# Products with w2 of 17 expert groups by one level of Strassen's algorithm

## The chip, the cores and the metric

The kernel runs on one core of a Trainium2 chip, in fp32 throughout. The metric is the device time of one execution in microseconds (us). The time before is the median of three executions. The profile is one execution, taken by the hardware profiler.

## The reference

One layer: a graph step with a dense 4096 x 4096 adjacency matrix, then a transformer block with a mixture of experts. The change concerns only the last loop.

```python
# x: 4096 x 256, adj: 4096 x 4096
x = x + gnn(layernorm(x), adj, neigh_W, lin_W)
x = x + ffn(layernorm(x), ...)          # the block below

# ffn: causal attention of 4 heads, then
flat = rmsnorm(x, ln2_w)                 # 4096 x 256
probs = softmax(flat @ router_w.T)       # 8 experts
tp, ti = top_k(probs, 2)                 # each token has two experts
for e in range(8):                       # hidden width 682
    hh = silu(flat @ w1[e].T) * (flat @ w3[e].T)
    out = out + weights[:, e:e+1] * (hh @ w2[e].T)
return x + out
```

## The kernel before

The kernel runs in three stages. First it multiplies the adjacency matrix with the features; there it already uses one level of Strassen's algorithm in Winograd's form, with the sums on VectorE (lines 374 to 377 and 444 to 450). Then it does attention with routing: each token's row is scattered into the list of each of its two experts. The third stage, from about 1109 us, does the experts, and the change is here.

Experts are worked off in groups of rows of one expert's list. There are 25 whole groups of 256 rows (numbers below `NW`) and 17 small ones of 128 rows that are done in the usual run. `TURNS` sets the order: nine whole groups first, then whole and small ones mixed so that each kind is spread evenly, then three whole ones. Written out, W for whole and s for small, from k = 0 to k = 41:

```
WWWWWWWWW sWsWsWssWsWsWsWssWsWsWssWsWsWs WWW
```

The program fixes the order on each engine by the order in which the code emits its instructions. For each k the main loop emits `hidden(k)`, then `combine(k - 1)`, with the loads of later groups between them.

`hidden(k)` makes 11 blocks of 128 hidden channels (5 of w1, 5 of w3, and one that holds both tails of 42 channels) from xT, the transposed rows, in three steps q = 0, 2, 4 with 8, 8 and 6 products (line 1105). Each step has its own PSUM pool of the three in `p_sc`. ScalarE takes silu (line 1111), VectorE multiplies (line 1112) into hT; the tail is multiplied last (line 1122). After the step q = 0 it calls `prepare(k + 1)`, which transposes the next group's rows (line 1083) into a tile tx of the pool `p_y` and copies it from there to xT on ScalarE (line 1088).

`combine(k)` multiplies hT and tail with w2 (line 1150): for each half of 128 rows six products, each with 128 channels of hT as stationary operand and 128 x 256 of w2 moving. Their sums lie in a tile ye of the pool `p_y`, which has a single buffer of one bank: tx and ye take turns in it. VectorE works out the gate (pick and gt, lines 1134 and 1138) and scales the sums to y (line 1161); GpSimd adds y to the rows in DRAM with an indirect DMA (line 1166). The last two groups use a bank of `p_ms` as well, one for each half.

One fp32 product shows as two matmul records in the profile.

Loads go through the queue of SyncE in the order of the code: for each k the weights w1 and w3 of k + 3 (`load13`, line 1053), the rows of k + 4 (`load_rows`, line 1069) and w2 of k + 2 (`load2`, line 1059). w13 and w2 have three places each; the rows have five buffers, of which one comes free when the scatter of its group has landed. `rest` holds what is left of routing and is worked off by `step()` in the first iterations.

Of the kernel before, what the change touches and what calls it, by code (L numbers as in the profile page):

```python
# [9 lines left out]
F32 = mybir.dt.float32  # L10
I32 = mybir.dt.int32
SP = mybir.EngineType.SP
AF = mybir.ActivationFunctionType
ALU = mybir.AluOpType
# [3 lines left out]
P = 128  # L18
N = 4096
C = 256  # L20
# [6 lines left out]
NF = 5  # L27
TAIL = HID - NF * P
T0 = 64
# [12 lines left out]
GR = 256  # L42
SM = 128
NA = -((NE * (GR - 1) - 2 * (N - 512)) // GR)
NW = -((NE * (GR - 1) - 2 * N) // GR)
# [8 lines left out]
NM = NG - RARE  # L54
# [12 lines left out]
def fast_kernel(  # L67
# [24 lines left out]
    nc = tc.nc  # L92
# [85 lines left out]
    kT = [kvp.tile([P, 512], F32, name=f"kT{b}") for b in range(NB)]  # L178
# [38 lines left out]
    with (  # L217
# [81 lines left out]
        T3 = G12  # L299
        HC = C // 2  # L300
# [230 lines left out]
    with (  # L531
# [259 lines left out]
                join(put, "late writes")  # L791


        def after(b):

            return [
                [None, lambda: inputs(b)],
                [None],
                [lambda: project(b, 0)],
                [lambda: project(b, 1)],  # L800
                [lambda: turn(b, 0)],
                [lambda: turn(b, 1), lambda: residual(b)],
                [lambda: logits(b)],
                [lambda: weigh(b)],
                [None, lambda: choose(b)],
                [None, lambda: scaled(b, 0)],
                [None, lambda: scaled(b, 1)],
                [lambda: place(b), lambda: scaled(b, 2)],
                [None, lambda: scaled(b, 3), lambda: scatter(b, 0, 0)],
                [None, lambda: scatter(b, 0, 1), lambda: scatter(b, 1, 0)],  # L810
                [None, lambda: scatter(b, 1, 1), lambda: scatter(b, 2, 0)],
                [None, lambda: scatter(b, 2, 1), lambda: scatter(b, 3, 0)],
                [None, lambda: scatter(b, 3, 1)],
            ]


        def last_qkv():
            b, made = NB - 1, {}

            def scales():  # L820
                stats(ax, b)
                var = mv[b][:, :, 1:2]
                power(rstd[b], var, 1.0, EPS_LN)
                power(both[b], var, *BOTH)

            def norm():
                made["h0"] = ax.tile([P, TB, ROW], F32, tag="row", name="h0_l")
                for t in range(TB):
                    normed(made["h0"][:, t, 0:C], b, t, both[b][:, t])

                made["hT"] = qT[b]

            def turned(h):
                tr = p_ms.tile([P, 2, 2, P], F32, tag="ms", name=f"tr_l{h}")
                for t in range(2):
                    for c in range(2):
                        nc.tensor.transpose(
                            tr[:, c, t, :], made["h0"][:, 2 * h + t, c * P : (c + 1) * P], ident
                        )
                for c in range(2):  # L840
                    nc.scalar.activation(
                        made["hT"][:, c, h * 2 * P : (h + 1) * 2 * P],
                        tr[:, c].rearrange("p t i -> p (t i)"),
                        AF.Copy, scale=ln1_sb[:, c : c + 1],
                    )

            def rotate(t):
                pj = p_ms.tile([P, 512], F32, tag="ms", name=f"pq_l{t}")
                room = ex.tile([P, NF, GR], F32, tag="hT", name=f"ro_l{t}")
                ro, r2 = (  # L850
                    room.rearrange("p k i -> p (k i)")[:, k : k + 384].rearrange(
                        "p (h s d) -> p h s d", s=2, d=HD // 2
                    )
                    for k in (0, 384)
                )
                rotated(ax, b, t, made["hT"], pj, ro, r2, cos_l[:, t, None, :], sin_l[:, t, None, :])
                made[t] = ro

            def turn_heads(t):
                tr = p_ms.tile([P, 2, 2, P], F32, tag="ms", name=f"trq_l{t}")  # L860
                heads(b, t, made.pop(t), tr)

            return [
                [None, scales], [None, norm], [lambda: turned(0)], [lambda: turned(1)],
                [lambda: rotate(0)], [lambda: rotate(1)],
                [lambda: turn_heads(0)], [lambda: rotate(2)],
                [lambda: turn_heads(1)], [lambda: rotate(3)],
                [lambda: turn_heads(2)], [lambda: turn_heads(3)],
                *guard(),
            ]  # L870
# [157 lines left out]
                join(put, "pads")  # L1028


        tails = [eg.tile([P, GR], F32, name=f"tail{n}") for n in range(2)]
        for t in tails:
            nc.gpsimd.memset(t, 0.0)

        at13 = (qT_all[:, 0 : 2 * W13], qT_all[:, 2 * W13 : 4 * W13], res_all[:, 0 : 2 * W13])
        W2 = (NF + 1) * C
        at2 = (
# [39 lines left out]
        def prepare(k, pool=p_y, tag="y"):  # L1077
# [13 lines left out]
                )  # L1091
            inputs_of[i] = xT

        def hidden(k, step=None, behind=None):
            i = TURNS[k]
            n = halves(i) * P
            w13_sb, xT = w13s[k % 3], inputs_of.pop(i)
            hT = ex.tile([P, NF, n], F32, tag="hT", name=f"hT_{i}")

            for q in range(0, NF + 1, 2):  # L1100
                ps = next(p_sc).tile([P, 2, 2, GR], F32, tag="sc", name=f"h_{i}_{q}")
                ps = ps[:, :, :, 0:n]
                for m in range(2 * q, min(2 * q + 4, 2 * NF + 1)):
                    for c in range(2):
                        nc.tensor.matmul(  # L1105
                            ps[:, m % 2, m // 2 - q, :], w13_sb[:, c, m * P : (m + 1) * P],
                            xT[:, c, :], start=(c == 0), stop=(c == 1),
                        )
                both = 2 if q + 1 < NF else 1
                si = ax.tile([P, 2, n], F32, tag="rden", name=f"si_{i}_{q}")  # L1110
                nc.scalar.activation(si[:, 0:both, :], ps[:, 0, 0:both, :], AF.Silu)  # L1111
                nc.vector.tensor_mul(  # L1112
                    hT[:, q : q + both, :], si[:, 0:both, :], ps[:, 1, 0:both, :]
                )
                if q == 0 and behind is not None:
                    prepare(behind)
                if step and q < NF - 1:
                    step()

            nc.scalar.activation(si[T0 : T0 + TAIL, 1, :], ps[0:TAIL, 0, 1, :], AF.Silu)  # L1120
            tail = tails[k % 2][:, 0:n]
            nc.vector.tensor_mul(
                tail[T0 : T0 + TAIL, :], si[T0 : T0 + TAIL, 1, :], ps[T0 : T0 + TAIL, 0, 1, :]
            )
            hidden_of[i] = (hT, tail)

        def combine(k):
            i = TURNS[k]
            n = halves(i)
            w2_sb = w2s[k % 3]  # L1130
            hT, tail = hidden_of.pop(i)
            r = rows.pop(i)
            pick = ex.tile([P, n, NE], F32, tag="pick", name=f"pick_{i}")
            nc.vector.tensor_mul(
# [4 lines left out]
            y = ax.tile([P, HALF, C], F32, tag="yT1", name=f"y_{i}")  # L1139

            last = k >= NM - 2
            ps = [
                pool.tile([P, HALF, C], F32, tag=tag, name=f"ye_{i}_{tag}")
                for pool, tag in ((p_ms, "ms"), (p_y, "y"))[0 if last else 1 :]
            ]

            def products(h):
                cols = slice(h * P, (h + 1) * P)
                for q in range(NF + 1):
                    nc.tensor.matmul(  # L1150
                        ps[h if last else 0][:, h, :],
                        hT[:, q, cols] if q < NF else tail[:, cols],
                        w2_sb[:, q, :], start=(q == 0), stop=(q == NF),
                    )

            for h in range(0 if last else n):
                products(h)
            for h in range(n):
                if last:
                    products(h)  # L1160
                nc.vector.tensor_scalar(  # L1161
                    y[:, h, :], ps[h if last else 0][:, h, :], gt[:, h], None, op0=ALU.mult
                )
                at = bass.IndirectOffsetOnAxis(ap=r[:, h, C : C + 1].bitcast(I32), axis=0)
                nc.gpsimd.memset(gap, 0.0)
                put = nc.gpsimd.indirect_dma_start(  # L1166
                    out=(acc_dram if k < NM - LAST else out)[:, :],
                    out_offset=at,
                    in_=y[:, h, :], in_offset=None, compute_op=ALU.add,
                )  # L1170
                if h:
                    free(put, f"half {i}", "an expert has a token once")
                else:
                    join(put, f"half {i}")
                if i < NA:
                    free(put, "last x", "the tokens of the first groups are others")
                    join(put, "first sums")
# [816 lines left out]
```

## Time and profile before

| | |
|---|---|
| time, median of three | 1638.8 us (1638.38 to 1639.15) |
| span of the profiled execution | 1636.5 us |
| TensorE busy | 1603.5 us |
| VectorE busy | 928.8 us |
| ScalarE busy | 457.9 us |
| line 1105, products of hidden(), wide groups' xT in qT_all | 220.5 us |
| line 1150, products with w2, largest row | 99.8 us |
| mean DMA rate | 128 GB/s |

How to read it: the engine rows are the union of the times in which at least one instruction of the engine ran; rows of a line likewise. TensorE is the engine with nearly no idle time. The chain of waits, followed back from the end, lies on PE for 88% of the span and on VectorE for 6%. Of the span, 10% are in this chain on line 1150. In the list of waits a line reads "engine, line, what it waited for: us in total, times, longest".

### The profile page before, as it was taken

What the parts mean: (1) busy time and instruction counts of PE and PEld (TensorE: products, weight loads), DVE (VectorE), ACT (ScalarE), POOL (GpSimd) and SP (SyncE); (2) the same over time, 40 slices, a digit from 0 to 9 for tenths busy, and PEclk for the clock granted to TensorE, in tenths of its full rate; (3) what the DMA queues carried; (4) which work ended last, traced back from release to release, by engine and by line L of the source; (5) the groups of instructions that cost most, each with busy time, mean ns of one, the idle gap of its engine ahead of it and who ended that gap; (6) DMA issues with size and microseconds to landing.
All of it is one profiled execution on the core that took longest, in us unless ns stands there. A gap on an engine that the chain in (4) does not pass through costs nothing.

```text
span 1636.5 us, 24754 instructions
## 1 busy us (share of the span) xinstructions
PE 1603.5 (98%) x9588; PEld 1157.6 (71%) x9588; DVE 928.8 (57%) x1914; ACT 457.9 (28%) x866; POOL 405.0 (25%) x604
## 2 busy tenths in 40 slices
PE   7999999999999999999999999999999999999997
PEld 5669999999999534344343434338888998999986
DVE  5647756756666578779778888793432222222221
ACT  2110000100000445555555455553211121221120
POOL 1001211111112221352434323412422222222122
PEclk9999999999999999999999999999999999999999
DMA  6224434434433000010001000066756777777765
GB/s 225 73 76 158 141 144 141 152 131 157 158 133 133 4 1 1 17 37 27 30 25 40 28 13 28 20 204 212 239 164 207 233 248 233 226 254 225 234 213 144
DMA packets 67711, 209.73 MB, mean 128 GB/s; under 512 B 14656, under 2 KB 46272, under 8 KB 53952
## 3 DMA queue, kind: packets, MB, share of 16 engines
q1 hardware_dynamic: 54320, 190.05, 33.4%
q0 software_dynamic: 12720, 17.47, 5.6%
q8 instruction: 78, 1.28, 0.3%
q10 hardware_dynamic: 544, 0.52, 0.1%
q14 instruction: 49, 0.40, 0.1%
HBM read 180.81 MB, written 31.42 MB: 130 GB/s over the span
## 4 chain that ended last, share of the span: by engine, by line
PE 88%; DVE 6%; issue 2%; ACT 2%; POOL 1%; DMA 1%; DVEq 0%; SPq 0%; ACTq 0%; POOLq 0%
PE acc L423 24%; PE h L1105 20%; PE ya L590 11%; PE sc L555 11%; PE ye_y L1150 10%; PE pf L385 3%; PE pq L184 3%; DVE sum L578 3%; PE po L624 2%; ACT pt L560 1%; PE tx L1083 1%; PE dn L603 1%; PE tr L318 1%; PE trq L212 1%; PE pq_l L184 0%
## 5 line engine op out<-in xcount | busy, mean ns | idle before, releaser
L560 ACT ACTIVATE pt<-sc 128x1024 f32<-128x1024 f32 (+3 forms) x288 | 251.8, 957 | 201.1 <-PE sc L555 162.5
L578 DVE TENSOR_TENSOR sum<-sum,pt 128x1024 f32<-128x1024 f32 (+3 forms) x258 | 294.3, 1141 | 20.4 <-POOL pt L562 0.5
L555 PE MATMUL sc<-qT_all,kT 64*128 64x512 f32 (+3 forms) x1152 | 253.3, 573 | 6.1 <-ACT pt L560 5.3
L423 PE MATMUL acc<-g,a 128*128 128x128 f32 x2048 | 255.7, 275 | 0.0
L590 PE MATMUL ya<-pt,vv 128*64 128x512 f32 (+3 forms) x1152 | 242.6, 563 | 0.0
L423 PEld LDWEIGHTS acc<-g,a 128*128 128x128 f32 x2048 | 241.8, 192 | 0.0
L1105 PE MATMUL h<-xT,qT_all 128*128 128x256 f32 (+1 forms) x1232 | 220.5, 335 | 0.0
L1112 DVE TENSOR_TENSOR hT<-si,h 128x256 f32<-128x256 f32 (+2 forms) x126 | 64.0, 508 | 261.1 <-ACT si L1111 261.1
L1105 PEld LDWEIGHTS h<-xT,qT_all 128*128 128x128 f32 x1232 | 194.2, 191 | 18.9 <-issue 1.0
L555 PEld LDWEIGHTS sc<-qT_all,kT 64*128 64x128 f32 x1152 | 104.2, 187 | 143.0 <-issue 105.1
L590 PEld LDWEIGHTS ya<-pt,vv 128*64 128x64 f32 x1152 | 76.3, 136 | 144.6 <-issue 138.7
L1166 POOL DMA_INDIRECT acc_dram<-y,rows x61 | 96.1, 1575 | 332.4 <-DVE y L1161 328.1
L1111 ACT ACTIVATE si<-h 128x256 f32<-128x256 f32 (+2 forms) x126 | 57.2, 454 | 376.3 <-PE h L1105 376.2
L1105 PE MATMUL h<-xT,res_all 128*128 128x256 f32 (+1 forms) x616 | 114.6, 342 | 0.0
L1105 PEld LDWEIGHTS h<-xT,res_all 128*128 128x128 f32 x616 | 100.3, 191 | 10.2 <-issue 0.2
L423 PE MATMUL acc<-g,more_sums 128*128 128x129 f32 (+1 forms) x768 | 101.7, 275 | 0.6 <-DVE more_sums L376 0.6
L423 PEld LDWEIGHTS acc<-g,more_sums 128*128 128x128 f32 x768 | 94.6, 192 | 7.5 <-issue 7.5
L1150 PE MATMUL ye_y<-res_all,hT 128*128 128x256 f32 x430 | 99.8, 379 | 0.0
L782 POOL DMA_INDIRECT lists<-row,slots x64 | 69.1, 1080 | 109.1 <-issue 106.5
L1150 PEld LDWEIGHTS ye_y<-res_all,hT 128*128 128x128 f32 x430 | 80.9, 190 | 10.5
L1161 DVE TENSOR_SCALAR y<-ye_y,gt 128x256 f32<-128x256 f32 x65 | 29.3, 481 | 86.1 <-PE ye_y L1150 86.0
L423 PE MATMUL acc<-g,qT_all 128*128 128x128 f32 (+1 forms) x512 | 74.0, 274 | 0.0
(231 smaller groups left out, 1716.5 us busy)
## 6 DMA issues: line engine op xcount, KB each, us to landing
a<-in_adj_dram SPq DMA_DIRECT2D x64, 1024.0 KB, 4.9
qT_all<-in_w_dram SPq DMA_DIRECT2D x28, 1408.0 KB, 8.2
res_all<-in_w_dram SPq DMA_DIRECT2D x28, 768.0 KB, 5.1
res_all<-in_w_dram SPq DMA_DIRECT2D x14, 1408.0 KB, 7.5
qT_all<-in_w_dram SPq DMA_DIRECT2D x14, 768.0 KB, 4.9
rows<-lists SPq DMA_DIRECT2D x25, 265.0 KB, 2.8
lists<-pad SPq DMA_DIRECT2D x8, 662.5 KB, 14.1
res_all<-in_x_dram SPq DMA_DIRECT2D x8, 512.0 KB, 9.4
```

The lines of the kernel that those rows point to most:

```text
L184: nc.tensor.matmul(pj, hT[:, c, t * P : (t + 1) * P], wqkv_sb[:, c, :], start=(c == 0), stop=(c == 1),)
L423: nc.tensor.matmul(acc[t][bank][:, at : at + w], m[left][:, k, t * P : (t + 1) * P], g[jb][:, right, k, 0:w], start=(jb == 0 and k == 0 an ...
L555: nc.tensor.matmul(ps[:, j, :w], kT[sb][hd, i * P : (i + 1) * P], qT[b][hd, p, off:], start=True, stop=True,)
L560: nc.scalar.activation(pt[:, :, :w], ps[:, :, :w], AF.Exp, scale=HD ** -0.5)
L578: nc.vector.tensor_add(sums[b, p][:, :, off:], before[:, :, off:], pt[:, :, : 512 - off])
L590: nc.tensor.matmul(accs[b, p][hd, off:], vv[sb][:, i, hd], pt[:, j, : 512 - off], start=(s == 0), stop=(s == TB * b + TB - 1),)
L782: put = nc.gpsimd.indirect_dma_start(out=lists[:, :], out_offset=bass.IndirectOffsetOnAxis(ap=chosen[b][:, k, t, :], axis=0), in_=flats[b] ...
L1105: nc.tensor.matmul(ps[:, m % 2, m // 2 - q, :], w13_sb[:, c, m * P : (m + 1) * P], xT[:, c, :], start=(c == 0), stop=(c == 1),)
L1111: nc.scalar.activation(si[:, 0:both, :], ps[:, 0, 0:both, :], AF.Silu)
L1112: nc.vector.tensor_mul(hT[:, q : q + both, :], si[:, 0:both, :], ps[:, 1, 0:both, :])
L1150: nc.tensor.matmul(ps[h if last else 0][:, h, :], hT[:, q, cols] if q < NF else tail[:, cols], w2_sb[:, q, :], start=(q == 0), stop=(q == NF),
L1166: put = nc.gpsimd.indirect_dma_start(out=(acc_dram if k < NM - LAST else out)[:, :], out_offset=at, in_=y[:, h, :], in_offset=None, comput ...
```

## The change

For 17 of the 25 whole groups (k = 6 to 39, where `TURNS[k] < NW`) the products with w2 are done by one level of Strassen's algorithm in Winograd's form. The matrix of 256 rows by 768 channels (six chunks of 128, the last one padded with zeros) is cut into four parts: by halves of rows and by even and odd chunks. w2 is cut by even and odd chunks and by halves of output channels. Seven products of three chunks each, 128 columns wide, take the place of eight; 15 sums on VectorE and one copy on ScalarE make this good.

- The tile hT gets a sixth chunk for the tail, and two fixed tiles hTs take the place of the rotating hT and of the tails. The rotation of the last block's heads borrows the same tiles.
- `split(k)`, at the end of `hidden(k)`, makes four sums of hT and four of w2, each 128 x (3 x 128), on VectorE. They lie in tiles of the attention stage that are no longer needed (kT and vv); two are written in place, over parts of hT and w2.
- `seven_products(k)`, in `combine(k)`, makes the products: four into a bank of `p_ms`, three into the one of `p_y`, and adds them up.
- The scaling of y with the gate goes to ScalarE for these groups.
- `prepare` of the next group moves from after q = 0 to after q = 2, in every group.

```diff
+        hTs = [eg.tile([P, NF + 1, GR], F32, name=f"hT{n}") for n in range(2)]
+        for t in hTs:
+            nc.gpsimd.memset(t[:, NF, :], 0.0)
...
-                room = ex.tile([P, NF, GR], F32, tag="hT", name=f"ro_l{t}")
+                room = hTs[t % 2]
...
-        tails = [eg.tile([P, GR], F32, name=f"tail{n}") for n in range(2)]
-        for t in tails:
-            nc.gpsimd.memset(t, 0.0)
...
+        SEVEN = [k for k in range(6, NM - 2) if TURNS[k] < NW]
+        def split(k, hT):
...
+                chunks = hT.rearrange("p (j c) i -> p c j i", c=2)[:, c]
+                weights = w2_sb.rearrange("p (j c) o -> p c j o", c=2)[:, c]
+                for h in range(2):
+                    m[f"A{h + 1}{c + 1}"] = chunks[:, :, h * P : (h + 1) * P]
+                    m[f"G{c + 1}{h + 1}"] = weights[:, :, h * P : (h + 1) * P]
+            first = k % 2 * 3
+            for n, s in enumerate(("S1", "S2", "S4")):
+                m[s] = kT[first + n][:, 0 : 3 * P].rearrange("p (j i) -> p j i", j=3)
+            for n, s in enumerate(("T1", "T2", "T4")):
+                m[s] = vv[first + n][:, 0:3, :]
+            m["S3"], m["T3"] = m["A21"], m["G12"]
+            nc.vector.tensor_add(m["S1"], m["A21"], m["A22"])
+            nc.vector.tensor_sub(m["S2"], m["S1"], m["A11"])
+            nc.vector.tensor_sub(m["S4"], m["A12"], m["S2"])
+            nc.vector.tensor_sub(m["S3"], m["A11"], m["A21"])
+            nc.vector.tensor_sub(m["T1"], m["G12"], m["G11"])
+            nc.vector.tensor_sub(m["T3"], m["G22"], m["G12"])
+            nc.vector.tensor_sub(m["T2"], m["G22"], m["T1"])
+            nc.vector.tensor_sub(m["T4"], m["T2"], m["G21"])
...
+        def seven_products(k):
...
+            banks = [
+                pool.tile([P, 4, HC], F32, tag=tag, name=f"ye_{i}_{tag}")
+                for pool, tag in ((p_ms, "ms"), (p_y, "y"))
+            ]
+            for number, left, right in (
+                (1, "A11", "G11"), (2, "A12", "G21"), (6, "S2", "T2"), (7, "S3", "T3"),
+                (5, "S1", "T1"), (3, "S4", "G22"), (4, "A22", "T4"),
+            ):
+                n = len(p)
+                p[number] = banks[n // 4][:, n % 4, :]
+                for j in range(3):
+                    nc.tensor.matmul(
+                        p[number], m[left][:, j, :], m[right][:, j, :],
+                        start=(n % 4 == 0 and j == 0), stop=(j == 2), skip_group_check=True,
+                    )
...
+            nc.scalar.copy(u2, p[1])
+            nc.vector.tensor_add(c[0][:, 0], u2, p[2])
+            nc.vector.tensor_add(u2, u2, p[6])
+            nc.vector.tensor_add(u3, u2, p[7])
+            nc.vector.tensor_add(u4, u2, p[5])
+            nc.vector.tensor_add(c[0][:, 1], u4, p[3])
+            nc.vector.tensor_sub(c[1][:, 0], u3, p[4])
+            nc.vector.tensor_add(c[1][:, 1], u3, p[5])
...
         def hidden(k, step=None, behind=None):
...
-                if q == 0 and behind is not None:
+                if q == 2 and behind is not None:
                     prepare(behind)
...
-            hidden_of[i] = (hT, tail)
+            hidden_of[i] = hT
+            if k in SEVEN:
+                split(k, hT)
...
         def combine(k):
...
+            if seven:
+                done = seven_products(k)
...
+                if seven:
+                    nc.scalar.activation(
+                        y[:, h, :], done[h].rearrange("p h o -> p (h o)"), AF.Copy, scale=gt[:, h]
+                    )
+                else:
+                    nc.vector.tensor_scalar(
+                        y[:, h, :], ps[h if last else 0][:, h, :], gt[:, h], None, op0=ALU.mult
+                    )
```

More of the change, by code (lines that the diff above doesn't have):

```diff
@@ L1092, in prepare @@
             inputs_of[i] = xT
+        SEVEN = [k for k in range(6, NM - 2) if TURNS[k] < NW]
+        parts_of = {}
+        def split(k, hT):
+            w2_sb = w2s[k % 3]
+            m = {}
+            for c in range(2):
+                chunks = hT.rearrange("p (j c) i -> p c j i", c=2)[:, c]
[17 more added lines that the diff above has]
+            nc.vector.tensor_sub(m["T4"], m["T2"], m["G21"])
+            parts_of[k] = m
@@ new lines, in seven_products @@
+        def seven_products(k):
+            i = TURNS[k]
+            m = parts_of.pop(k)
+            HC = C // 2
+            banks = [
+                pool.tile([P, 4, HC], F32, tag=tag, name=f"ye_{i}_{tag}")
+                for pool, tag in ((p_ms, "ms"), (p_y, "y"))
+            ]
+            p = {}
+            for number, left, right in (
[9 more added lines that the diff above has]
+                    )
+            c = [vv[6 + k % 2].rearrange("p (r h) o -> p r h o", r=2)[:, r] for r in range(2)]
+            u2 = u4 = c[0][:, 1]
+            u3 = c[1][:, 1]
+            nc.scalar.copy(u2, p[1])
[6 more added lines that the diff above has]
+            nc.vector.tensor_add(c[1][:, 1], u3, p[5])
+            return c
@@ L1097, in hidden @@
             w13_sb, xT = w13s[k % 3], inputs_of.pop(i)
-            hT = ex.tile([P, NF, n], F32, tag="hT", name=f"hT_{i}")
+            hT = hTs[k % 2][:, :, 0:n]
             for q in range(0, NF + 1, 2):
@@ L1120, in hidden @@
             nc.scalar.activation(si[T0 : T0 + TAIL, 1, :], ps[0:TAIL, 0, 1, :], AF.Silu)
-            tail = tails[k % 2][:, 0:n]
             nc.vector.tensor_mul(
-                tail[T0 : T0 + TAIL, :], si[T0 : T0 + TAIL, 1, :], ps[T0 : T0 + TAIL, 0, 1, :]
+                hT[T0 : T0 + TAIL, NF, :], si[T0 : T0 + TAIL, 1, :], ps[T0 : T0 + TAIL, 0, 1, :]
             )
-            hidden_of[i] = (hT, tail)
+            hidden_of[i] = hT
+            if k in SEVEN:
+                split(k, hT)
         def combine(k):
@@ L1130, in combine @@
             w2_sb = w2s[k % 3]
-            hT, tail = hidden_of.pop(i)
+            hT = hidden_of.pop(i)
             r = rows.pop(i)
@@ L1141, in combine @@
             last = k >= NM - 2
[L1142 to L1145, printed above, removed]
+            seven = k in SEVEN
+            if seven:
+                done = seven_products(k)
+            else:
+                ps = [
+                    pool.tile([P, HALF, C], F32, tag=tag, name=f"ye_{i}_{tag}")
+                    for pool, tag in ((p_ms, "ms"), (p_y, "y"))[0 if last else 1 :]
+                ]
             def products(h):
@@ L1151, in products @@
                         ps[h if last else 0][:, h, :],
-                        hT[:, q, cols] if q < NF else tail[:, cols],
-                        w2_sb[:, q, :], start=(q == 0), stop=(q == NF),
+                        hT[:, q, cols], w2_sb[:, q, :], start=(q == 0), stop=(q == NF),
                     )
-            for h in range(0 if last else n):
+            for h in range(0 if last or seven else n):
                 products(h)
@@ L1160, in combine @@
                     products(h)
-                nc.vector.tensor_scalar(
-                    y[:, h, :], ps[h if last else 0][:, h, :], gt[:, h], None, op0=ALU.mult
-                )
+                if seven:
+                    nc.scalar.activation(
+                        y[:, h, :], done[h].rearrange("p h o -> p (h o)"), AF.Copy, scale=gt[:, h]
+                    )
+                else:
+                    nc.vector.tensor_scalar(
+                        y[:, h, :], ps[h if last else 0][:, h, :], gt[:, h], None, op0=ALU.mult
+                    )
                 at = bass.IndirectOffsetOnAxis(ap=r[:, h, C : C + 1].bitcast(I32), axis=0)
```

## The prediction

> **What bounds the kernel now.** I read the engine table of the page first, then its clock row, then the list of who waited for whom, then the timeline of the stretch that the change touches.
>
> ```profile
> PE 1603.5 (98%) x9588; PEld 1157.6 (71%) x9588; DVE 928.8 (57%) x1914; ACT 457.9 (28%) x866; POOL 405.0 (25%) x604
> PEclk9999999999999999999999999999999999999999
> ```
>
> TensorE is busy 98% of the span at full clock. In the expert stage (from about 1180 us) the list of waits has no entry of PE or PEld at all. So here each us that TensorE is spared comes off the time, and each us that it is made to wait goes on it. What matters is not the share of VectorE (a quarter in this stage: 86.5 of the 343.1 us from 1246.4 to 1589.5) but where its work stands in its order. One pair of a small and a whole group, timeline of before (start, length, engine, line, operation; a count of weight loads on PEld):
>
> ```profile
> 1350.91 2.03 PEld L1150 LDWEIGHTS ye_y<-res_all,hT 128*128 128x128 f32 x10
> ...
> 1355.98 3.43 PEld L1105 LDWEIGHTS h<-xT,qT_all 128*128 128x128 f32 x16
> ...
> 1356.40 0.88 DVE L1161 TENSOR_SCALAR y<-ye_y,gt 128x256 f32<-128x256 f32 x2 [3.55 <-PE ye_y L1150]
> ...
> 1365.70 2.13 PEld L1150 LDWEIGHTS ye_y<-qT_all,hT 128*128 128x128 f32 x10
> ...
> 1367.39 0.42 DVE L1122 TENSOR_TENSOR tail<-si,h 42x256 f32<-42x256 f32 x1 [0.44 <-ACT si L1120]
> 1367.85 0.17 DVE L1134 TENSOR_TENSOR pick<-rows,mine 128x8 f32<-128x8 f32 x1
> ...
> 1368.05 0.16 DVE L1138 TENSOR_REDUCE gt<-pick 128x1 f32<-128x8 f32 x1
> ...
> 1368.29 1.97 PEld L1105 LDWEIGHTS h<-xT,res_all 128*128 128x128 f32 x16
> ...
> 1368.71 0.48 DVE L1161 TENSOR_SCALAR y<-ye_y,gt 128x256 f32<-128x256 f32 x1 [0.49 <-PE ye_y L1150]
> ...
> 1370.18 0.47 PEld L1083 LDWEIGHTS tx<-ident,rows 128*128 128x128 f32 x4
> ...
> 1374.42 0.38 SPq L1069 DMA_DIRECT2D rows<-lists  x1
> ...
> 1375.04 0.33 SPq L1059 DMA_DIRECT2D qT_all<-in_w_dram  x1
> ```
>
> The reader is to see four things. (a) The 24 matmul records of a whole group's w2 products (12 products, two records each) hold TensorE from 1350.91 to 1355.98, 5.07 us; after a stretch of wide products it is 5.18 (1196.07 to 1201.25). (b) hidden() of the whole group ends at 1365.70, the small group's w2 products end at 1368.29. (c) VectorE multiplies the whole group's tail at 1367.39, and only then comes the small group's pick, gt and y; y, at 1368.71 to 1369.19, empties the one bank of p_y. (d) tx, which writes the same bank, begins at 1370.18, 0.99 us after y let it go. That 0.99 us is the slack the change spends.
>
> The rate of 128-wide products is read from the adjacency stage, where the kernel already multiplies in this form (four records to a line):
>
> ```profile
> 312.02 0.52 PEld L423 LDWEIGHTS acc<-g,qT_all 128*128 128x128 f32 x4
> 312.47 0.53 PEld L423 LDWEIGHTS acc<-g,a 128*128 128x128 f32 x4
> 312.91 0.53 PEld L423 LDWEIGHTS acc<-g,qT_all 128*128 128x128 f32 x4
> ```
>
> Four take 0.445 us, so 111.3 ns each, against 213.3 ns for a 256-wide one (10 and 2 of them between 1353.39 and 1355.98 fit that). Halving the width doesn't quite halve the price. The pace of VectorE, from the same stage:
>
> ```profile
> 302.58 0.69 DVE L375 TENSOR_TENSOR qT_all<-qT_all,a 128x512 f32<-128x512 f32 x1
> 303.31 0.69 DVE L376 TENSOR_TENSOR kT<-a,qT_all 128x512 f32<-128x512 f32 x1
> 303.92 0.69 DVE L377 TENSOR_TENSOR a<-a 128x512 f32<-128x512 f32 x1
> ...
> 306.96 0.29 DVE L448 TENSOR_TENSOR vv<-vv,acc 128x128 f32<-128x128 f32 x1
> 307.16 0.28 DVE L449 TENSOR_TENSOR vv<-vv,acc 128x128 f32<-128x128 f32 x1
> 307.48 0.29 DVE L450 TENSOR_TENSOR vv<-vv,acc 128x128 f32<-128x128 f32 x1
> ```
>
> From start to start a sum that needs the one just ahead takes 0.73 us at 512 elements and 0.32 at 128; one that doesn't takes 0.61 and 0.20. On a straight line through these, 384 elements take 0.59 and 0.47.
>
> [...] y of a whole group's first half starts at 1356.40, after the last product of both halves, though its own were through about 2.5 us earlier.
>
> **Part 1, the products.** Each of the 17 groups loses 24 records of 213.3 ns, 5.12 us, and gets 7 x 3 products of two records, 42 x 111.3 ns = 4.67 us. The bare gain is 0.45 us. The new products wait for more producers; the old ones lose about 0.06 us to that (5.18 against 5.12), and I allow 0.03 more: 0.42 us, 17 x 0.42 = 7.1 us. Bounds 6.0 and 7.7.
>
> **Part 2, split().** Eight sums of 128x384 on VectorE, after the tail product and, in VectorE's order, ahead of pick, gt and y of the group before and of the next hidden()'s multiplications. The order S1, S2, S4, S3, T1, T3, T2, T4 has three that need the one just ahead and five steps (the last being to pick) that don't: 3 x 0.59 + 5 x 0.47 = 4.1 us. No page row shows 128x384 between SBUF tiles, so bounds: 8 x 0.47 = 3.8 and 8 x 0.59 = 4.7. The 17 splits are 70 us of VectorE in a stage where it is three quarters idle; what counts is who stands behind.
>
> **Part 3, prepare() at q == 2.** It must wait for the bank of p_y. Take the pair above and put the split in. The tail ends at 1367.81, S1 starts at 1367.84, pick at 1371.98, y at 1372.37 (0.39 from pick to y's readiness, as at 1367.85 to 1368.24), y ends at 1372.85. TensorE sees it about 0.05 later: 1372.90. TensorE comes to tx after the small group's first two thirds, 32 records of 111.3 ns from 1368.29 (the first load comes at the pace of the 213 ns record before it): 1371.96. It stands for 0.94 us[...]: 1.0 us. At the old place, q == 0, it would have been 2.8. With the bounds of part 2: 0.6 and 1.5. Nothing else runs on TensorE meanwhile, as its products come in order.
>
> How often: the group after a whole one of the 17 must be small (a whole one gives 32 x 213.3 ns = 6.8 us before tx, which is enough). From TURNS, the small groups stand at k = 9, 11, 13, 15, 16, 18, 20, 22, 24, 25, 27, 29, 31, 32, 34, 36, 38, so these are k = 8, 10, 12, 14, 17, 19, 21, 23, 26, 28, 30, 33, 35, 37. Thirteen have a small group ahead too and are the pair above: 13.0 us. At k = 8 the group ahead is one of the seven-product ones; its products keep TensorE 2.1 us longer, but seven reads of PSUM at 0.20 to 0.39 us (2.2 us) replace y: about 0.4 us. In all 13.4 us.
>
> **Part 4, unloading.** A copy on ScalarE and seven sums on VectorE take the place of two tensor_scalars of 0.48, and y moves to ScalarE, 2 x 0.4 us. Both banks are free 1.3 us after the last product (four more reads of the y bank); tx then comes 3.7 us (small) or 6.8 us (whole) after it, so the following hidden() hides this. ScalarE stands for the sums with the next silu behind it, and has three buffers of sc to make that good: nothing.
>
> **Part 5, loads.** Row loads wait for the scatter of an earlier group (the buffer rows), with the w2 load queued behind them. A y that is 3.7 us later makes the w2 load that much later: 9.3 us after hidden()'s end becomes 13.0, and with the 5.1 us to landing that the page gives, 18.1. T1 of the next whole group's split, its first reader now, comes at 13.7 + 9.7 + 2.1 + 2.1 = 27.6. Hidden. The merged hT and tail tiles, the memsets and the rotation's room change no amount of work: nothing.
>
> **Sum.** -7.1 + 13.4 = +6.3 us: 1645.1 us. The end of the program is unchanged: the last two groups keep their products, and the copy to out, some 4 us later behind k = 39's split, ends before the last scatters want it.
>
> **Rivals.** (A) The split is hidden and the gain stands whole: 1638.8 - 7.1 = 1631.7. For it: VectorE idles three quarters of this stage, and q == 2 gives TensorE more room than q == 0. Against it: it needs y 1 us earlier than the sum of measured paces, or the sums interleaved with pick and y. (B) The stall is half as long, 0.5 us, because [...] the start of hidden() is later than read: -7.1 + 6.9, 1638.6, no change. (C) Each of the 17 also waits elsewhere, for S2 and T2, for the banks, or for w2: 0.5 us x 17 more, 1653.6. For it: more producers per product; against: six us or more of slack in each of those.
>
> **How the numbers follow.** Forecast (stall of 0.75 to 1.5 us) 0.62, A 0.19, B 0.12, C 0.07. Slower by over 0.2% (3.3 us) are forecast and C nearly whole: 0.68; faster is A with a little of B: 0.20; the rest, 0.12, is no change. Bounds of the stall (0.6 to 1.5, thirteen times) with those of the gain give 1639 to 1652.5; leaving out A whole and C would be over 2 in 10, so the range goes down to the edge of A: 1632 to 1652.
>
> **What would show it.** Right: waits of PE for DVE y at tx (line of prepare()), some 14 of about 1 us; L1150's successor at 111 ns a record; split of 3.8 to 4.7 us. Wrong: no such wait, tx starting freely in small groups; or waits of the seven products for sums or for a DMA, which would be C; or 128-wide products slower than 111 ns.

## The result and the profile after

The changed kernel takes 1649.0 us (median of six, 1647.6 to 1649.9), the kernel before 1638.6 us beside it. The ratio is 1.0061, with a 95% interval of 1.0048 to 1.0074: slower by some 10 us. The forecast was 1645.1 us and slower, in a range of 1632 to 1652.

The page's engine table and clock row, of the changed kernel:

```profile
PE 1599.1 (97%) x9894; PEld 1160.2 (70%) x9894; DVE 1014.1 (62%) x2135; ACT 480.9 (29%) x917; POOL 405.8 (25%) x604
PEclk9999999999999999999999999999999999999998
```

TensorE is busy 4.4 us less although the span is 10.9 us longer. So it does less work and stands still for more time. The list of waits of the weight loads, from 1180 us on, names where (it had no entry before):

```profile
PEld tx L1084 <- DVE y L1239: 14.0, 13, 1.2
PEld tx L1084 <- DVE vv L1160: 0.6, 1, 0.6
```

Thirteen waits of about 1.1 us, and one of 0.6 at k = 8: the places and nearly the sizes that the prediction listed. One pair of groups, in the timeline after (this is the stretch shown of before; prepare() is now line 1084, hidden()'s products 1174, the tail 1190, pick and gt 1204 and 1208, y 1239):

```profile
1368.31 2.56 PEld L1224 LDWEIGHTS ye_y<-qT_all,hT 128*128 128x128 f32 x12
...
1370.01 0.42 DVE L1190 TENSOR_TENSOR hT<-si,h 42x256 f32<-42x256 f32 x1 [0.44 <-ACT si L1189]
1370.46 0.56 DVE L1118 TENSOR_TENSOR kT<-hT 128x384 f32<-128x384 f32 x1
1370.90 3.76 PEld L1174 LDWEIGHTS h<-xT,res_all 128*128 128x128 f32 x32
...
1374.24 0.56 DVE L1125 TENSOR_TENSOR vv<-vv,res_all 128x384 f32<-128x384 f32 x1
1374.72 0.16 DVE L1204 TENSOR_TENSOR pick<-rows,mine 128x8 f32<-128x8 f32 x1
...
1375.17 0.48 DVE L1239 TENSOR_SCALAR y<-ye_y,gt 128x256 f32<-128x256 f32 x1
...
1375.70 0.42 PEld L1084 LDWEIGHTS tx<-ident,rows 128*128 128x128 f32 x4 [1.05 <-DVE y L1239]
...
1377.43 1.42 PEld L1146 LDWEIGHTS ye_ms<-res_all,hT 128*128 128x128 f32 x12
...
1380.46 0.48 SPq L1060 DMA_DIRECT2D qT_all<-in_w_dram  x1
...
1382.12 6.78 PEld L1174 LDWEIGHTS h<-xT,qT_all 128*128 128x128 f32 x32
...
1391.74 1.27 PEld L1224 LDWEIGHTS ye_y<-res_all,hT 128*128 128x128 f32 x6
```

The reader is to see the queue on VectorE. The sums run from 1370.46 to 1374.72; the small group's pick, gt and y follow them, where in the kernel before they came right after the tail. TensorE has come to tx at about 1374.6 and loads its weights only at 1375.70, 50 ns after y has emptied the bank. The seven products take 4.69 us (1377.43 to 1382.12). The pair lasts from 1368.31 to the same point of the next pair at 1391.74, 23.43 us; before it was 22.83 (1350.91 to 1373.74). So each such pair is 0.6 us longer: less on the products, more at tx.

The end differs too. Timeline of before, then after, of the copy of acc_dram to out (SPq) and of some of the scatters into out (POOL) that follow:

```profile
1594.47 0.60 SPq L1267 DMA_DIRECT2D out_dram<-acc_dram  x1
...
1612.42 1.57 POOL L1166 DMA_INDIRECT out_dram<-y,rows  x1 [0.19 <-issue]
...
1617.87 1.57 POOL L1166 DMA_INDIRECT out_dram<-y,rows  x1 [3.77 <-DVE y L1161]
...
1621.87 2.13 PEld L1150 LDWEIGHTS ye_y<-res_all,hT 128*128 128x128 f32 x10
```

```profile
1606.46 0.60 SPq L1345 DMA_DIRECT2D out_dram<-acc_dram  x1
...
1624.67 1.57 POOL L1244 DMA_INDIRECT out_dram<-y,rows  x1 [0.19 <-issue]
1624.77 0.48 DVE L1239 TENSOR_SCALAR y<-ye_ms,gt 128x256 f32<-128x256 f32 x1 [0.47 <-PE ye_ms L1224]
...
1629.53 2.56 PEld L1224 LDWEIGHTS ye_y<-res_all,hT 128*128 128x128 f32 x12
...
1629.72 1.57 POOL L1244 DMA_INDIRECT out_dram<-y,rows  x1 [3.37 <-issue]
```

Before, the scatter of k = 40 (1617.87) went off when its y was made. After, its y is made at 1625.25 (0.48 us from 1624.77), yet the scatter goes off at 1629.72, 5.05 us after the last one of k = 39. Those of k = 39 had queued behind the copy: their y was ready at 1614.35, the first of them went off at 1622.79, 16.33 us after the copy's issue (16.08 before, 1594.47 to 1610.55). From the first load of the last twelve products to the end of the span it was 14.6 us (1621.87 to 1636.5); now it is 17.9 (1629.53 to 1647.4).

### The profile page after: what moved, and what is told of

Read it like the earlier page. It is cut to its first block, busy times and chain, and to the rows that moved or that the text cites. A ratio compares the mean times of both kernels' runs of the same rounds, so it can differ in the third digit from the quotient of the medians.

```text
span 1647.4 us, 25656 instructions
## 1 busy us (share of the span) xinstructions
PE 1599.1 (97%) x9894; PEld 1160.2 (70%) x9894; DVE 1014.1 (62%) x2135; ACT 480.9 (29%) x917; POOL 405.8 (25%) x604
## 5 line engine op out<-in xcount | busy, mean ns | idle before, releaser
L562 POOL TENSOR_SCALAR_AFFINE_SELECT pt<-pt 128x256 f32<-128x256 f32 x64 | 39.5, 640 | 137.9 <-ACT pt L560 129.4
L423 PEld LDWEIGHTS acc<-g,qT_all 128*128 128x128 f32 x512 | 66.5, 192 | 7.2 <-issue 7.2
L198 POOL TENSOR_TENSOR ro<-ro,r 128x192 f32<-128x192 f32 x28 | 16.5, 590 | 218.6 <-DVE r L195 218.6
```

The lines of the kernel that those rows point to most:

```text
L198: nc.gpsimd.tensor_sub(ro[:, :, 0, :], ro[:, :, 0, :], r2[:, :, 0, :])
L423: nc.tensor.matmul(acc[t][bank][:, at : at + w], m[left][:, k, t * P : (t + 1) * P], g[jb][:, right, k, 0:w], start=(jb == 0 and k == 0 an ...
L562: nc.gpsimd.affine_select(out=pt[:, :, 0:P], in_=pt[:, :, 0:P], pattern=[[0, 2], [1, P]], compare_op=ALU.is_ge, fill=0.0, base=0, channel_ ...
```

## The experiments

Two theories stood against each other. Mine: the change gains about 7 us on the products, loses 14 us because y stands behind split() on VectorE while tx waits for y's bank, and 3 us at the end from the late copy. The rivals: the products or their unloading are what is slow, or the later prepare() is, or VectorE's backlog holds TensorE in other ways too.

**e1_move**, the one edit of prepare()'s place in the kernel before:

```diff
-                if q == 0 and behind is not None:
+                if q == 2 and behind is not None:
```

> The kernel before with one edit of the change: prepare() after q == 2. Theory (the changed kernel loses 14 us to waits of tx for y behind split(), and some 3 us at the end to the late copy of acc_dram to out): without split() the bank of p_y is free well before q == 2, no wait, 1638.6 us, within 1. Rival (the later place itself costs, since xT comes later and the next hidden() waits for it): several us above 1640, with waits of h for xT.

Measured: 1639.2 us against 1638.9 of before, ratio 1.0001 (0.9993 to 1.0009), and no wait of TensorE from 1180 us on. From the first load of hidden(0) to the first of the last twelve products both traces take 512.89 us, so the move alone costs nothing there.

**e2_no_sums**, the products without the eight sums:

```diff
-            nc.vector.tensor_add(m["S1"], m["A21"], m["A22"])
-            nc.vector.tensor_sub(m["S2"], m["S1"], m["A11"])
...
-            nc.vector.tensor_sub(m["T4"], m["T2"], m["G21"])
```

> The changed kernel without the eight sums of split(); the seven products read what lies in their tiles, so this part of the computation is left out. Theory: no waits at tx, no late copy at the end, the bare gain of the products stays: 1638.6 - 7.1 = 1631.5 us. Rival (42 records of 128 columns with their waits are no cheaper than 24 of 256, and the slowing is theirs): 1638 to 1649.

Measured: 1631.1 us, ratio 0.9950 (0.9936 to 0.9964), no wait of TensorE. The gain of the products is there, 7.8 us by the medians. From the first load of hidden(0) to the first of the last twelve products it is 8.33 us (504.56 against 512.89), so their unloading and y on ScalarE cost TensorE nothing there. This rival falls. What was expected of the end didn't hold: the copy is late here too (24.43 us ahead of the last twelve products, 27.40 before; more on this under e4_split_late), and from the last twelve products to the end of the span it takes 15.8 us, not 14.6.

**e3_sums**, the sums without the products:

```diff
-            m["S3"], m["T3"] = m["A21"], m["G12"]
+            m["S3"] = kT[6 + k % 2][:, 0 : 3 * P].rearrange("p (j i) -> p j i", j=3)
+            m["T3"] = vv[6 + k % 2][:, 0:3, :]
...
-            seven = k in SEVEN
+            seven = False
```

> The changed kernel with the eight sums of split() kept (S3 and T3 written to two more free tiles instead of in place, nothing reads any of them) and the 12 old products of 256 columns in place of the seven. Theory: 13 waits of tx for y of about 1.1 us (none at k = 8, where y now comes before q == 2 ends) and the late copy, but no gain: 1649.0 + 7.1 - 0.5 = about 1655.5 us. Rival (the sums are hidden, the loss is in the products or their unloading): 1638.6.

Measured: 1655.2 us, ratio 1.0099 (1.0084 to 1.0115). Its list of waits of the weight loads has thirteen waits and none for k = 8:

```profile
PEld tx L1084 <- DVE y L1240: 12.3, 13, 1.3
```

The sums cost 16.3 us by themselves (1655.2 - 1638.9), of which 12.3 are these waits; the end, 17.7 us where before has 14.6, makes 3.1 more.

**e4_split_late**, the same work with split() behind y:

```diff
             hidden_of[i] = hT
-            if k in SEVEN:
-                split(k, hT)
...
                 combine(k - 1)
                 step()
+            if k in SEVEN:
+                split(k, hidden_of[TURNS[k]])
```

> The changed kernel with split(k) emitted after combine(k - 1), so pick, gt and y of the group before come ahead of the sums on VectorE. Theory: no wait at tx, the copy to out as early as before, and the sums (4.3 us) still done before the third of the seven products at the end of the next hidden(): 1638.6 - 7.1 = 1631.5 us. Rival (the sums now hold up the multiplications of the next hidden(), and TensorE waits for those instead, or for S2 and T2): 1640 to 1649, with waits of h or ye for DVE.

Measured: 1630.7 us, ratio 0.9948 (0.9935 to 0.9962), with no wait of TensorE from 1180 us on. Timeline of a pair:

```profile
1342.76 0.48 DVE L1237 TENSOR_SCALAR y<-ye_y,gt 128x256 f32<-128x256 f32 x1 [0.49 <-PE ye_y L1222]
1343.16 0.55 DVE L1118 TENSOR_TENSOR kT<-hT 128x384 f32<-128x384 f32 x1
...
1346.02 0.47 PEld L1084 LDWEIGHTS tx<-ident,rows 128*128 128x128 f32 x4
...
1346.93 0.56 DVE L1125 TENSOR_TENSOR vv<-vv,res_all 128x384 f32<-128x384 f32 x1
1347.41 0.74 DVE L1181 TENSOR_TENSOR hT<-si,h 128x256 f32<-128x256 f32 x2
...
1349.14 0.75 PEld L1146 LDWEIGHTS ye_ms<-vv,kT 128*128 128x128 f32 x6
```

The sums now run beside tx and beside hidden()'s products, and end at 1347.49, 1.65 us before the first product that reads one. The next hidden()'s multiplications do wait for them (1347.41), but TensorE has another bank for each step and doesn't. From the first load of hidden(0) to the first of the last twelve products this kernel takes 504.56 us, to the last digit what e2_no_sums takes without any sums. So the same sums, in the same number, hold TensorE for 12.7 us in one place of the order (e3_sums, 525.63 against 512.89) and for nothing in the other.

One part of what was expected didn't hold: the copy isn't as early as before. Timeline of the scatter of k = 38 and what follows:

```profile
1581.90 0.48 DVE L1237 TENSOR_SCALAR y<-ye_y,gt 128x256 f32<-128x256 f32 x1 [0.49 <-PE ye_y L1222]
...
1585.06 1.94 POOL L1242 DMA_INDIRECT acc_dram<-y,rows  x1 [10.19 <-DVE vv L1122]
...
1589.19 0.60 SPq L1345 DMA_DIRECT2D out_dram<-acc_dram  x1
...
1613.38 2.56 PEld L1222 LDWEIGHTS ye_y<-res_all,hT 128*128 128x128 f32 x12
```

The scatter goes off 2.68 us after its y (1582.38), where before it was 0.28 (1590.39 to 1590.67). The line names a sum of split(), but the scatter doesn't read it, and e2_no_sums, without sums, has the same delay (2.80 us). In both the second scatter of k = 37 landed late, 11.2 and 10.3 us after its issue against 7.1 before, which fits the delay; why it landed late wasn't traced. The copy goes out 24.19 us ahead of the last twelve products, 27.40 before, and the end takes 16.8 us, not 14.6. So some 2 us of the gain are still lost at the end.

**e5_skip39**, the last of the 17 groups left out:

```diff
-        SEVEN = [k for k in range(6, NM - 2) if TURNS[k] < NW]
+        SEVEN = [k for k in range(6, NM - 3) if TURNS[k] < NW]
```

> The changed kernel with k = 39, the last of the 17, left with its twelve old products, so that no split() stands ahead of the y of k = 38, whose scatter the copy to out waits for. Theory (the end costs 3.3 us by itself: the copy starts 3.7 us later after the last hidden() groups than before, and the scatters into out queue behind it): 1649.0 - 3.3 + 0.4 = 1646.1 us, and the last products are again followed by 12 us, not 15. Rival (the end is as long as before and all of the loss is in the middle): 1649.4.

Measured: 1646.3 us, ratio 1.0042 (1.0028 to 1.0055); its waits at tx are those of the changed kernel (14.0 us, 13 times, and 0.6). 2.6 us less than the changed kernel, for one group less. The two kernels weren't run beside each other and the intervals of their ratios are each over 4 us wide, so by the times alone the size is uncertain. The traces settle it: the copy goes out 27.48 us ahead of the last twelve products (1602.22 and 1629.70), as before, and from there to the end of the span it takes 14.9 us, against 17.9 in the changed kernel and 14.6 before. What split() of this group does is delay the copy: the y of k = 38, and with it the copy, comes some 3.8 us later after the start of hidden(40) in the changed kernel than before.

**e6_other_bank**, another bank for tx where split() runs ahead of y:

```diff
-                    prepare(behind)
+                    prepare(behind, *((p_ms, "ms") if k - 1 in SEVEN else ()))
...
-                for pool, tag in ((p_ms, "ms"), (p_y, "y"))
+                for pool, tag in ((p_y, "y"), (p_ms, "ms"))
```

> The changed kernel with tx in the bank of p_ms whenever the group ahead of hidden()'s group is one of the 17, and the seven products' two banks changed over (four in p_y, then three in p_ms). split() stays where it is. Theory (the wait is for the bank alone): no wait of tx for y of a small group, k = 8 and the late copy stay: 1649.0 - 13.5 = 1635.5 us. Rival (VectorE's backlog behind the sums would hold TensorE anyway, through the multiplications or the products' operands): 1642 to 1649, with waits for other tiles.

Measured: 1635.3 us, ratio 0.9975 (0.9966 to 0.9984). The one wait left is that of k = 8:

```profile
PEld tx L1084 <- DVE vv L1160: 0.6, 1, 0.6
```

In its timeline tx now comes ahead of y, behind the same sums:

```profile
1346.42 0.56 DVE L1125 TENSOR_TENSOR vv<-vv,res_all 128x384 f32<-128x384 f32 x1
1346.76 0.47 PEld L1084 LDWEIGHTS tx<-ident,rows 128*128 128x128 f32 x4
...
1347.47 0.48 DVE L1239 TENSOR_SCALAR y<-ye_y,gt 128x256 f32<-128x256 f32 x1 [0.21 <-PE tx L1084]
```

VectorE is as late as in the changed kernel, and TensorE doesn't mind. The wait was for the bank. From the first load of hidden(0) to that of the last twelve products it takes 505.17 us, which is e4_split_late's 504.56 and the wait of k = 8. The end, with the copy late as in the changed kernel, takes 18.9 us.

**e7_q0**, prepare() back at its old place:

```diff
-                if q == 2 and behind is not None:
+                if q == 0 and behind is not None:
```

> The changed kernel with prepare() back after q == 0. Theory: each of the 13 waits grows by the 16 records of q == 2, 1.78 us, and that of k = 8 likewise; the whole groups now wait as well at k = 7 (0.9) and k = 39 (1.3): 14 x 1.8 + 2.2 = 27 us more, about 1676 us. Rival (the waits aren't set by the place of prepare()): 1649.

Measured: 1692.6 us, ratio 1.0324 (1.0310 to 1.0338), against the 1676 that I expected. The waits are as worked out, 41.8 us against 14.6, 27.2 more:

```profile
PEld tx L1084 <- DVE y L1239: 38.5, 14, 3.0
PEld tx L1084 <- DVE vv L1160: 3.3, 2, 2.4
```

The other 16 us were not foreseen; the last section deals with them.

**e8_more**, e4_split_late with two more groups:

```diff
-        SEVEN = [k for k in range(6, NM - 2) if TURNS[k] < NW]
+        SEVEN = [k for k in range(4, NM - 2) if TURNS[k] < NW]
```

> split(k) after combine(k - 1), as in e4_split_late, and two more groups, k = 4 and 5, by seven products. Theory: 0.42 us less for each, 1630.7 - 0.8 = 1629.9 us, hardly to be told from e4_split_late. Rival (routing's last steps on VectorE are still under way at k = 4, and the sums run into them): 1631 to 1633.

Measured: 1629.5 us, ratio 0.9941 (0.9927 to 0.9955). By the times that isn't to be told from e4_split_late. By the traces the stretch from hidden(0) to the last twelve products is 0.98 us shorter (503.58 against 504.56), 0.49 for each group. Both beat both kernels, by about 0.5% against before and over 1% against the changed one.

## Why the prediction was right, and where it was not

- **The products** (7.1 us gained, bounds 6.0 and 7.7). Right in kind, a little small. The sets of 21 take 4.69 us by the trace, near the 4.67 of the bare rate, where a set of 12 took 5.18 (5.07 in the pair shown, where the first load comes at the pace of the narrow record before it: 2.05 us for the first ten records, 1350.91 to 1352.96, and 2.16 for the ten of the second half, 1353.39 to 1355.55); the 0.09 us set aside for waits of the new products were 0.02. That is 0.49 us a group, 17 x 0.49 = 8.3, above the upper bound, and e2_no_sums and e4_split_late are 8.33 us shorter in this stretch. (By the times they gained 7.8 and 8.2, each with an interval that holds 7.1.)
- **split()** (4.1 us). Right: from S1 to pick it takes 4.26 us, within the bounds. The straight line between 128 and 512 elements, with one pace for sums that need their forerunner and one for those that don't, gave 0.59 and 0.47; the trace has 0.60 (1370.46 to 1371.06) and 0.47 (1372.13 to 1372.60). What was left out: T3, in place over what T1 reads, also came at the slower pace (0.58, 1372.60 to 1373.18).
- **The wait at tx** (13 x 1.0 and 0.4). Right in place and number, 1.08 us and 0.6 in size, 14.6 us for 13.4. (Of the 1.0, 0.94 came from the trace's paces, the rest was my estimate.) Against e4_split_late the stretch is 15.0 us longer (519.59 and 504.56). e6_other_bank shows that the wait is for the bank, e4_split_late that it comes of the order, e1_move that the move isn't part of the cost.
- **Unloading and loads** (nothing). Right: e2_no_sums has them, and TensorE has no wait. The w2 load goes out 12.15 us after hidden()'s end in the pair shown (1368.31 to 1380.46), near the 13.0 worked out, and nothing waits for it.
- **The end** ("unchanged", since the copy would end before the last scatters want it). This step failed. The prediction has the delay of the copy, some 4 us, but works out no slack for the scatters behind it: the two of k = 39 stand between the copy and those of the last two groups, and the first of a group goes off some 5 us after the last of the group ahead even when its y is ready (5.05 and 4.68 in the changed kernel). In the changed kernel the copy goes out 23.07 us ahead of the last twelve products, where it was 27.40, so 4.3 us later (3.8 by split(), 0.5 because the products of k = 39 are shorter). From the copy to the end of the span it takes 40.9 us, where it was 42.0 with waits for y in between, so this chain had 1.1 us of slack. That leaves the 3.2 us that the end grew by (17.9 against 14.6, unrounded 17.87 and 14.63), and e5_skip39 shows that the delayed copy is the cause.

The sum: from the first load of hidden(0) (1108.98 and 1109.94) to the first of the last twelve products TensorE took 512.89 us before and 519.59 after, +6.7 where +6.3 was forecast. That nearness is in part luck: 1.2 us more were gained on the products and 1.6 us more lost at tx than forecast. +3.2 come from the end. The 1.0 us left of the 10.9 lies ahead of the experts, where the start of hidden(0) varies from 1108.8 to 1110.9 us among the profiles of kernels with the same work up to there; it isn't put down to the change. Of the rivals, A's 1631.7 us is what e4_split_late reaches (1630.7): it is the change with its work in another place.

## What to carry to other kernels

Before work is moved to an engine that has time, look at what stands behind it in that engine's order and which buffer that work would have freed: 4.3 us of sums on a VectorE that idled three quarters of the stage before cost 1.1 us of TensorE in thirteen places, because a 0.5 us read of a single-buffered bank came after them. First try another place in the order or another bank: here either took the thirteen waits away, and the other place in the order eased the end as well (1630.7 us against 1635.3). A copy or scatter chain at the end deserves the same sum as the main loop: add up its links from the first to the end of the program, and compare the slack that they leave with the delay.

## What the runs showed of the hardware that was not expected

In e7_q0 TensorE stands still for 2.8 us at a time, and then mostly runs at half clock, 0.50, for 3.4 us. Timeline of its weight loads at one such place:

```profile
1392.03 0.42 PEld L1084 LDWEIGHTS tx<-ident,rows 128*128 128x128 f32 x4 [2.83 <-DVE y L1239]
1392.41 4.83 PEld L1174 LDWEIGHTS h<-xT,res_all 128*128 128x128 f32 x28
```

The 28 records take 4.76 us (to the next load at 1397.17), 170 ns each, where they take 111 otherwise (3.12 us). The view by stretches of the same run (stretch, length, busy time of weight loads, then the granted clock):

```profile
1384.60:1389.00 4.40, 4.04 (x28) 1.00 0.93 351
1392.00:1393.00 1.00, 0.97 (x8) 0.78 0.00 0
1393.00:1394.00 1.00, 1.00 (x7) 0.50 0.00 0
1394.00:1395.00 1.00, 1.00 (x6) 0.50 0.65 57
1395.00:1396.00 1.00, 1.00 (x6) 0.51 0.48 74
1396.00:1397.00 1.00, 1.00 (x11) 1.00 0.00 0
```

The clock is 0.50 from about 1392.6, shortly after the stop, until about 1396; over the four rows from 1392 to 1396 that makes 3.4 us at half clock (0.44 + 1 + 1 + 0.98). This happens after ten of the fourteen waits of 2.4 to 3.0 us, that of k = 8 among them, and not after four of 2.8 to 3.0; the stretch of 28 records then takes 4.2 to 4.8 us instead of 3.2. That is 14.9 us in all (the lengths of the ten stretches less 3.21 each), most of the 16 that the waits don't explain. The mean granted clock of the whole run is 0.985, where the changed kernel has 0.994.

The kernel before has the same length of half clock at one place, at the start of attention: TensorE stands still for 4.17 us (to 550.44), and in the four us from 550 the granted clock is 0.68, 0.50, 0.50 and 0.62, 3.4 us at half clock. The changed kernel has 6.8 us of it there (549 to 556), at a stop of 4.18 us. The length of the stop alone doesn't decide: in e7_q0 one of 2.37 us (to 1251.61) was hit, with 4.83 us for the 28 records, and one of 2.85 (to 1278.46) wasn't, with 3.21. What does decide, the runs don't show. The waits of the changed kernel, 1.1 us, left the clock at 1.00 in every 10 us from 1220 to 1620. So here a wait that grew from 1.1 to 2.8 us cost up to 1.6 us on top of its growth (4.83 less 3.21).
